# A planned two-layer kernel: own memory for the scans' rows, streamed first-expert weights, and a re-timed plan

## The chip, the cores and the metric

The kernel runs on one core of a Trainium2 chip. The metric is the time of one execution on the device, in microseconds; times of several runs are given by their median. A profile shows one execution in detail.

The engines are named as in the profile: PE (matrix multiply, with PEld for its weight loads), DVE (vector), ACT (activations), POOL (GpSimd), and SP, which here only issues DMA transfers. Each engine runs its own instructions in their order and waits for the others by semaphores.

## The reference, cut to what matters

Sixteen batches of 256 tokens with 128 features go through two layers. Each layer has an attention-like part and experts; norms, shifts, scales and gates stand around them.

```python
# layer 0, attention part: retention with 8 heads, decay g per head
S = g * S + k_t[..., :, None] * v_t[..., None, :]
y_t = einsum('bhde,bhd->bhe', S, q_t)            # then a group norm and Wo
# layer 0, experts: each of 8 experts chooses 64 tokens of each batch
top_p, top_idx = top_k(softmax(x @ gate_w)ᵀ, 64)
y = gelu(xin @ w1) @ w2 * top_p                  # added back to the chosen tokens
# layer 1, attention part: a selective scan, 256 channels x 16 states
dA = exp(dt_t[..., None] * A)
h = dA * h + dt_t[..., None] * b_t[:, None, :] * u_t[..., None]
y = einsum('bdn,bn->bd', h, c_t)                 # + u*D, times silu(z), W_out, layer norm
# layer 1, experts: each token chooses 2 of 8 experts
out = sum_k weight_k * (silu(x @ w1_k) * (x @ w3_k)) @ w2_k
```

All of it is float32.

## The kernel before

**The planner.** The kernel is not written in its final order. Each piece of work is a *chain* of operations with an urgency (`pl.chain(U[...])`, lower numbers first). A chain can `need` results, `take` tokens that stand for buffers, and `give` them back. `Plan.issue` keeps a clock for each engine and repeatedly chooses the next operation: of those that could start within 0.15 us of the earliest one on that engine, the one of the most urgent chain. The order in which it emits them becomes the fixed order of each engine. The durations that it uses come from the formulas of `_us`, or from a `us=` at the call; a DMA's time to land from `_lag`. It plays no part on the chip: at run time only the order and the semaphores remain. Nearly all operations are recorded through one helper, so most have line L119 in the profile and are told apart by tile names.

**Retention** (`retention(g)`, four groups of four batches). `scores` makes the norm, `pqk`, `pv`, and four score tiles `sc` with products `pr`; `outputs0` makes `py` and `yT`; `project` makes `po`; `expert_scores` makes `gs`; `choose` runs eight rounds of `V.max` and `match_replace` on `wk` and ends with `done(("slot", g))`. The scores of the four `j` use four PSUM banks of their own (`ps_d`'s two, `ps_c`, `ps_y`).

**First experts** (`experts_of(q)`, four passes of four batches). `gather` builds one-hot `gg` and `px`; `hidden` multiplies with `fw1` into `ph` and applies gelu to `hg`; `outputs` multiplies with `fw2` into `pye` and copies to `ysb`; `scatter` reads rows `gt` and `pr` from DRAM and adds `pos` to the residual, ending with `done(("x0", b))`. `fw1` and `fw2` are loaded once, 2 MB each, from ACT's queue, and stay in memory.

**Scans.** `front(b)` makes the norm, `bt`, `pxs`, `u`, `pdt` and the softplus, and writes `dx` to DRAM as `dd`. `scans()` holds 256 units, 16 for each batch. Per pair of units SP reads a 512 KB row tile `rep` (three buffers). ACT makes `dA` (exponential, two PSUM tiles), POOL `dB` (twelve buffers), DVE the scan `h` and its product with `ct` (written over `dB`), and PE sums eight products at a time into `ya`. `back(k)` makes `pom`, its layer norm `om`, and the residual (`x1`).

`begin()` opens the memory pool `ml` of the scans' rows after closing the retention's pool, and runs `scans` and `back`; it is hooked on the last group's choice:

```python
pl.after([("slot", 3)], begin)
```

**Second experts.** `prepare(k)` makes `ph`, `hs`, `gbh` and the logits `pl`; `route(g)` ranks tokens (groups of batches (0-3), (4-7), (8-13), (14-15)); `send(g)` scatters rows `disp` by indirect DMA from POOL; `expert(g, j)` works on 128-row tiles, 92 in all: `xt`, `px`, `pa`, `pg`, `sl`, `pm`, `mT`, `py`, `yt`, `ydr`; `combine(k)` gathers `got` and writes `acc`. The weights `w1`, `w3`, `w2` are loaded in `second()`, which is hooked on all `x0`.

Of the kernel before, what the change touches and what calls it, by code (L numbers as in the profile page):

```python
# [31 lines left out]
U = dict(A=-15, AS=0.05, setup=-15.2, E=(-15.5, -12.700000000000001, -13.3, -10.2), Eh=-0.5, Eo=1.5, norm=-16,  # L32
         front=-15, gates=-14, rep=-20, exp=-20, dB=-18.5, ct=-20, sum=-20, scan=5, yg=-16, back=-15, prep=-22,
         route=-22, send=-28.0, tile=-12, comb=-11, wts=-20, depth=2, gap=1.3, wlag=25)
# [58 lines left out]
class Plan:  # L93
# [15 lines left out]
    def _engine(self, key, real):  # L109
        plan = self  # L110

        class Engine:
            def __getattr__(self, name):
                def call(*args, us=None, lag=None, **kw):
                    if us is None:
                        us = plan._us(key, name, args, kw)
                    if lag is None:
                        lag = plan._lag(name, args, kw)
                    return plan.op(key, us, lambda: getattr(real, name)(*args, **kw), lag)  # L119

                return call

        return Engine()
# [139 lines left out]
def adaln_two_layers(ctx: ExitStack, tc: tile.TileContext, a: dict, out: bass.AP):  # L263
# [25 lines left out]
    pe = phase.enter_context(tc.tile_pool(name="pe", bufs=1, side="right"))  # L289

    ma = ctx.enter_context(tc.tile_pool(name="ma", bufs=1))
# [56 lines left out]
    fw1 = fixed(r1, [P, E, HF], "fw1")  # L348
    fw2 = fixed(r1, [P, E, 4, D], "fw2")
    iota0 = fixed(r1, [P, CAP], "iota0")  # L350
    slot_tok = fixed(r1, [P, NCH, B, E], "slot_tok")
    lcol = fixed(r1, [P, 1], "lcol")
# [35 lines left out]
    pl.tokens(hTa=4, an=8, xna=2, q=2, v=2, kd=1, pr0=1, pr1=1, pr2=1, pr3=1, yT=6, tabA=4, yn=2, res=1)  # L388
    pl.tokens(w=2, e=2, va=1, vg=1, vx=1, vy=1, ct=2, ya=1)
    pl.tokens(xin=4, xnq=1, gg=2, gt=2, pr=1, hg=2, ysb=4, fres=1, tab0=1, fn=2)  # L390
    pl.tokens(hT=5, bt=3, th=1, u=3, dx=1, spy=1, spl=1, sz=2, yg=2, om=1)
    pl.tokens(xn2=1, hTf=1, sq=1, hs=4, hs0=2, gbh=1, tab1=1, tab2=1, tab3=1, acc=1, got=3)
# [75 lines left out]
    def retention(g):  # L468
# [17 lines left out]
        own = ((ps_d, "dA0", "va"), (ps_d, "dA1", "vg"), (ps_c, "c", "vx"), (ps_y, "y", "vy"))  # L486
        side = "e"
# [3 lines left out]
        up = U['A'] + U['AS'] * g  # L491
        p_tok = at.tile([P, NCH, 4, E], F32, tag="p_tok", name=f"p_tok{g}")

        def feature_major(b, which, nb, rs, i, name):
# [4 lines left out]
            take("hTa", 2)  # L499
# [21 lines left out]
        def scores(b):  # L521
# [13 lines left out]
            give("hTa")  # L535
# [29 lines left out]
            take(side)  # L565
            T_.matmul(pk[:, 0, :], hT[:, 0:P], wk, start=True, stop=True, us=0.25)
# [33 lines left out]
        def outputs0(b):  # L600
# [17 lines left out]
            yT = yTs[b] = at.tile([P, L], F32, tag="yT", name=f"yT{b}", bufs=6)  # L618
# [38 lines left out]
        def project(b):  # L657
# [4 lines left out]
            yn = at.tile([P, L], F32, tag="yn", name=f"yn{b}")  # L662
# [16 lines left out]
        def expert_scores(g):  # L679
# [5 lines left out]
            for i in range(4):  # L685
# [8 lines left out]
                give("hTa", "hTa")  # L694
# [61 lines left out]
    pl.chain(-20)  # L756
    need(("an", 0))
    S.dma_start(fw1, a["fw1"].rearrange("p (e h) -> p e h", e=E), us=0.35)
    S.dma_start(fw2, a["fw2"].rearrange("p (e h c) -> p e h c", e=E, h=4), us=0.35)
# [129 lines left out]
    def gather(b):  # L889
# [21 lines left out]
        take("w")  # L911
# [10 lines left out]
        give("w")  # L922
        done(("xin", b))

    def hidden(q):
# [8 lines left out]
        for e in range(E):  # L934
            for hp in range(2):
                pool, tag, tok = own[2 * (e % 2) + hp] if q == 0 else (ps_w, "w", "e")
                ph = pool.tile([P, 2, 4 * CAP], F32, tag=tag, name=f"ph{q}_{e}_{hp}")
                banks[e, hp] = ph, tok
            for hp in range(2):
                take(banks[e, hp][1])  # L940
                for hh in range(2):
                    hc = 2 * hp + hh
                    T_.matmul(
                        banks[e, hp][0][:, hh, :], fw1[:, e, hc * P : (hc + 1) * P],
                        xin[:, e].rearrange("p b l -> p (b l)"), start=True, stop=True, us=0.43,
                    )
            done(("ph", q, e))
# [12 lines left out]
    def outputs(q):  # L960

        for ep in range(4):
# [3 lines left out]
            ysb = ysbs[q, ep] = rf.tile([P, 4, D], F32, tag="ysb", name=f"ysb{q}_{ep}", bufs=4)  # L966
            take("ysb")
            take("w")
            for bi in range(4):
                for hc in range(4):  # L970
                    for e2 in range(2):
                        T_.matmul(
                            py[e2 * CAP : (e2 + 1) * CAP, bi, :],
                            hgs[q, 2 * ep + e2][:, hc, bi * CAP : (bi + 1) * CAP], fw2[:, 2 * ep + e2, hc, :],
                            start=(hc == 0), stop=(hc == 3), us=0.127,
                        )
            give("hg", "hg")
# [4 lines left out]
    def scatter(q):  # L982
# [3 lines left out]
        tab = tab0s[q] = rf.tile([P, 4, D], F32, tag="tab0", name=f"tab0_{q}")  # L986
        take("tab0")
        Q.dma_start(tab, rowd0[4 * q : 4 * q + 4, D : 2 * D].unsqueeze(0).to_broadcast([P, 4, D]))
        for bi in range(4):
            b = 4 * q + bi  # L990
            gt = gts[b] = rf.tile([P, 4, L], F32, tag="gt", name=f"gt{b}", bufs=2)
            pr = rf.tile([P, 4, L], F32, tag="pr", name=f"pr{b}", bufs=1)
            if b:
                need(("gt", b - 1))
            take("gt")
            take("pr")
            for i, t in enumerate((gt, pr)):
                for e2 in range(2):
                    rows = spd[b // 4].rearrange("(b e k) (i t) -> i b k e t", e=4, k=2, i=2)[i, b % 4, e2]
                    Q.dma_start(t[e2 * CAP : (e2 + 1) * CAP], rows.unsqueeze(0).to_broadcast([CAP, 4, L]), lag=9.0)  # L1000
            V.scalar_tensor_tensor(gt, gt, lcol, pr, ALU.is_equal, ALU.mult, us=1.3)
            give("pr")
            done(("gt", b))
        pl.chain(U['E'][q] + U['Eo'])
        for bi in range(4):
            b = 4 * q + bi
            need(("gt", b), *(("ysb", q, ep) for ep in range(4)))
            po = mbank([P, NCH, D], f"pos{b}")
            take("w")
            for ch in range(NCH):  # L1010
                for ep in range(4):
                    T_.matmul(
                        po[:, ch, :], gts[b][:, ep, ch * P : (ch + 1) * P], ysbs[q, ep][:, bi, :], start=(ep == 0), stop=(ep == 3),
                        us=0.24,
                    )
            give("gt")
            if bi == 3:
                give("ysb", "ysb", "ysb", "ysb")
            t = rf.tile([P, NCH, D], F32, tag="fres", name=f"fres{b}")
            take("fres")  # L1020
            V.tensor_tensor(t, po, both(tab[:, bi, :]), ALU.mult)
            give("w")
# [8 lines left out]
    def front(b):  # L1031
# [10 lines left out]
        hT = hTs[b] = ma.tile([P, DC - 1 + L], F32, tag="hTm", name=f"hTm{b}", bufs=5)  # L1042
# [10 lines left out]
        bt = bts[b] = ma.tile([P, 2, L], F32, tag="bt", name=f"bt{b}", bufs=3)  # L1053
# [220 lines left out]
    def prepare(k):  # L1274
# [30 lines left out]
        for i in range(2):  # L1305
# [4 lines left out]
            if i == 1:  # L1310
                give("w")
# [367 lines left out]
```

## Time and profile before

| what | value |
|---|---|
| three runs, us | 1384.59, 1396.2, 1391.0 (median 1391.0) |
| the profiled execution | 1367.15 us, span 1365.4 us |
| mean granted TensorE clock | 0.873 |
| PE busy | 1054.5 us, 77% |
| DVE busy | 933.8 us, 68% |
| ACT busy | 772.2 us, 57% |
| POOL busy | 760.0 us, 56% |
| moved by DMA | 143.45 MB, mean 105 GB/s |
| scan steps `h` | first at 330.6 us, last at 1128.9 us |

The span runs from the first to the last instruction; the execution's own time has a little more around it. The median of the three runs is 1.7% above the profiled execution, so differences within the profile are to be read against its own 1367.15 us. Busy shares are averages over stages with different limits; the prediction cuts the span into stages.

### The profile page before, as it was taken

Reading aid. Unit: us, or ns where it says so; the run is one execution under the profiler, and the core shown is the slowest. Engines: PE = TensorE matmul, PEld = TensorE weight load, DVE = VectorE, ACT = ScalarE, POOL = GpSimd, SP = SyncE. Lnnn points to the kernel's source line nnn. Section 1 sums busy time; section 2 is a strip of 40 time slices with the busy share of each in tenths; the row PEclk is TensorE's granted clock in tenths of the full one; section 3 lists DMA queues with packets and bytes.
Section 4 is the critical chain, followed back from the end, with each engine's and each line's share of the span. In section 5 each row is a group of like instructions: output and inputs, shape, how many; then the busy total and the mean of one; then the engine's idle time right before and its main releaser. Section 6 shows DMA issues by size and latency. Waiting matters only on the chain.

```text
span 1365.4 us, 20311 instructions
## 1 busy us (share of the span) xinstructions
PE 1054.5 (77%) x6227; PEld 711.7 (52%) x6227; DVE 933.8 (68%) x1844; ACT 772.2 (57%) x1641; POOL 760.0 (56%) x1241
## 2 busy tenths in 40 slices
PE   5997999988777778577645778777668768889993
PEld 4776678666546545255422444445334445556662
DVE  3576545644888888676995989988899894533341
ACT  2344453256659766668455666667776553444452
POOL 3223112134565776857786877878768876450074
PEclk9898898799879988888875988988798899989997
DMA  8124300323547457333667534535435431221132
GB/s 265 14 68 120 72 11 1 72 70 95 131 117 170 108 128 166 83 84 102 171 173 212 143 102 118 157 87 148 120 106 148 111 104 54 64 80 39 38 94 58
DMA packets 108442, 143.45 MB, mean 105 GB/s; under 512 B 15864, under 2 KB 86592, under 8 KB 107712
## 3 DMA queue, kind: packets, MB, share of 16 engines
q1 hardware_dynamic: 102800, 122.06, 34.7%
q0 software_dynamic: 4256, 9.18, 2.4%
q10 hardware_dynamic: 1280, 10.90, 2.2%
q8 instruction: 53, 0.87, 0.3%
q14 instruction: 53, 0.43, 0.1%
HBM read 115.06 MB, written 27.04 MB: 104 GB/s over the span
## 4 chain that ended last, share of the span: by engine, by line
PE 32%; DVE 25%; POOL 15%; ACT 11%; issue 8%; DMA 7%; DVEq 0%; POOLq 0%; ACTq 0%; SPq 0%
DVE h L119 9%; POOL dB L119 5%; DMA rep<-dd 5%; DVE dB L119 4%; PE py L1494 3%; PE pa L1464 3%; ACT L119 3%; PE sc L119 3%; ACT dA L119 3%; PE pg L1464 3%; PE pxs L119 2%; PE ya L119 2%; PE py L119 2%; DVE sl L119 2%; PE pye L119 2%
## 5 line engine op out<-in xcount | busy, mean ns | idle before, releaser
L119 POOL TENSOR_TENSOR dB<-rep,bt 128x512 f32<-128x512 f32 x256 | 326.7, 1296 | 132.7 <-DMA rep<-dd 74.3
L119 DVE TENSOR_TENSOR_SCAN h<-dA,dB 128x512 f32<-128x512 f32 x256 | 314.7, 1229 | 75.9 <-ACT dA L119 54.5
L119 ACT ACTIVATE dA<-rep,A 128x255 f32<-128x255 f32 x512 | 241.5, 476 | 152.4 <-DVE h L119 138.4
L119 DVE TENSOR_TENSOR dB<-h,ct 128x512 f32<-128x512 f32 x256 | 176.2, 688 | 6.5
L119 PE MATMUL ya<-dB,c 128*32 128x512 f32 x512 | 87.2, 724 | 65.5 <-DVE dB L119 65.3
L1494 PE MATMUL py<-w,mT 112*128 x736 | 106.9, 291 | 31.0 <-ACT mT L119 25.2
L1494 PEld LDWEIGHTS py<-w,mT 112*128 112x128 f32 x736 | 96.3, 199 | 63.8 <-ACT mT L119 37.7
L119 POOL DMA_INDIRECT got<-ydr,pos x64 | 61.5, 961 | 109.7 <-ACT mT L119 78.1
L119 DVE SCALAR_TENSOR_TENSOR sl<-sl,pa 128x448 f32<-128x448 f32 x92 | 56.6, 615 | 90.6 <-ACT sl L119 90.6
L1464 PE MATMUL pa<-w,xT 128*128 x184 | 97.8, 616 | 15.3 <-DVE sl L119 5.9
L119 ACT ACT_TABLE_LOAD x74 | 94.9, 1283 | 1.3
L1464 PE MATMUL pg<-w,xT 128*128 x184 | 92.8, 588 | 0.3 <-DVE sl L119 0.3
L119 PE MATMUL ph<-xin,fw 128*128 128x256 f32 x256 | 70.3, 421 | 21.9 <-ACT hg L119 11.8
L1412 POOL DMA_INDIRECT disp<-hs,pos x64 | 64.1, 1001 | 32.4 <-DVE pos L119 16.6
L119 PE MATMUL pye<-fw,hg 128*64 128x128 f32 x1024 | 73.4, 297 | 6.7 <-ACT dx L119 3.2
L119 PE MATMUL pxs<-hTm,wcv 128*128 128x256 f32 x256 | 77.7, 448 | 0.0
L119 ACT COPY mT<-pm 112x512 f32<-112x512 f32 x92 | 53.5, 583 | 37.0 <-PE pm L119 36.9
L119 PEld LDWEIGHTS pye<-fw,hg 128*64 128x64 f32 x1024 | 64.0, 150 | 18.5 <-issue 6.6
L119 PEld LDWEIGHTS ya<-dB,c 128*32 128x32 f32 x512 | 15.9, 124 | 107.8 <-DVE dB L119 75.1
L119 PE MATMUL pm<-c,sl 128*112 128x128 f32 x368 | 59.5, 283 | 15.0 <-DVE sl L119 9.8
L119 PEld LDWEIGHTS ph<-xin,fw 128*128 128x128 f32 x256 | 51.3, 210 | 36.1 <-ACT hg L119 14.0
L119 POOL TENSOR_TENSOR qd<-q,c 128x128 f32<-128x128 f32 x16 | 7.6, 473 | 107.6 <-ACT q L119 107.6
(293 smaller groups left out, 2213.5 us busy)
## 6 DMA issues: line engine op xcount, KB each, us to landing
rep<-dd SPq DMA_DIRECT2D x128, 512.0 KB, 4.5
gt<-spd SPq DMA_DIRECT2D x32, 256.0 KB, 4.8
pr<-spd SPq DMA_DIRECT2D x32, 256.0 KB, 5.7
dd<-dx SPq DMA_DIRECT2D x16, 512.0 KB, 3.8
xt<-disp SPq DMA_DIRECT2D x92, 64.0 KB, 1.9
ydr<-yt SPq DMA_DIRECT2D x92, 64.0 KB, 1.8
w<-in_w ACTq DMA_DIRECT2D x3, 1792.0 KB, 17.3
fw<-in_fw ACTq DMA_DIRECT2D x2, 2048.0 KB, 8.5
```

The source lines that it names most:

```text
L119: return plan.op(key, us, lambda: getattr(real, name)(*args, **kw), lag)
L1412: i = nc.gpsimd.indirect_dma_start(out=disp[g], out_offset=bass.IndirectOffsetOnAxis(ap=pos[g][:, c, r, :], axis=0), in_=hss[GROUPS[g][c / ...
L1464: nc.tensor.matmul(o, xT, w[:, bass.ds(which[0], 1), :].rearrange("p o i -> p (o i)"), start=True, stop=True)
L1494: nc.tensor.matmul(py, mT[:, ic, :], w2[:, bass.ds(which[0], 1), ic, :].rearrange("p o d -> p (o d)"), start=(ic == 0), stop=(ic == NFC - 1),)
```

## The change

The change touches where buffers lie, which event opens the scans, how the first experts' weights arrive, which tiles are copied out of PSUM, and the planner's numbers.

1. The scans' pool `ml` is opened beside the retention's from the start. `scans` and `back` move from `begin` to a new `recur`, hooked on the scores of retention group 1 (`EARLY = 2`) and all `hg` of pass 0. Retention groups 2 and 3 use the shared PSUM pool `ps_w` with the two tokens `e` for their scores.
2. `fw1` and `fw2` become 32 tiles each per kernel (expert by expert, for each of the four passes), 256 KB apiece, loaded from SP, with 2 and 4 buffers.
3. `ysb`, `tab0`, `gt`, `pr`, `fres` lie in a pool `rw` that the second experts share for `hs`, `acc`, the tables and `got`. `gt` and `pr` are halved. Buffers of `yT` go from 6 to 4, `yn` 2 to 1, `hTm` 5 to 4, `bt` and `u` 3 to 2.
4. `om` and `hs` are copied out of PSUM by ACT first; statistics, `gbh` and `hs` then read the copy.
5. `w1` and `w3` are loaded in `begin`, `w2` in `second`, which is hooked on the last pass's `ysb`.
6. The planner looks up durations in a table `USUAL` by engine, tile and size, and all urgencies `U` are new.

```diff
-U = dict(A=-15, AS=0.05, setup=-15.2, E=(-15.5, -12.700000000000001, -13.3, -10.2), Eh=-0.5, Eo=1.5, norm=-16,
-         front=-15, gates=-14, rep=-20, exp=-20, dB=-18.5, ct=-20, sum=-20, scan=5, yg=-16, back=-15, prep=-22,
-         route=-22, send=-28.0, tile=-12, comb=-11, wts=-20, depth=2, gap=1.3, wlag=25)
+U = dict(A=(-27.35, -16.05, -15.45, 46.6), setup=-34.65, E=(-42.15, 39.3, 75.0, 33.85), Eh=-43.75, Eo=-49.25,
+         norm=34.2, front=-6.85, gates=-73.15, rep=-27.35, exp=-15.05, dB=91.6, ct=32.55, sum=6.05, scan=87.0,
+         yg=38.9, back=-20.75, prep=-42.55, route=12.25, send=-52.55, tile=23.35, comb=38.9, wts=23.25,
+         depth=2, gap=1.3, wlag=25, fw=27.7)
+
+USUAL = {
+    "S": {("A", 32): 0.189, ("xna", 128): 0.411, ("hTa", 256): 0.515, ("q", 256): 0.355, ("ko", 256): 0.444,
...
+                    us = USUAL.get(key, {}).get((short, out.free_size()), us)
                     return plan.op(key, us, lambda: getattr(real, name)(*args, **kw), lag)
...
     ma = ctx.enter_context(tc.tile_pool(name="ma", bufs=1))
+    ml = ctx.enter_context(tc.tile_pool(name="ml", bufs=2))
+
+    rw = ctx.enter_context(tc.tile_pool(name="rw", bufs=1))
...
-    fw1 = fixed(r1, [P, E, HF], "fw1")
-    fw2 = fixed(r1, [P, E, 4, D], "fw2")
+
+    NF1, NF2 = 2, 4
+    fw1s, fw2s = {}, {}
...
+    EARLY = 2
+    TPX, TPO = "w", "w"
+    NYT, NHT, NBT, NU, NGT = 4, 4, 2, 2, 3
...
         own = ((ps_d, "dA0", "va"), (ps_d, "dA1", "vg"), (ps_c, "c", "vx"), (ps_y, "y", "vy"))
+        if g >= EARLY:
+            own = ((ps_w, "w", "e"),) * 4
...
-    pl.chain(-20)
+    pl.chain(U['fw'])
     need(("an", 0))
-    S.dma_start(fw1, a["fw1"].rearrange("p (e h) -> p e h", e=E), us=0.35)
-    S.dma_start(fw2, a["fw2"].rearrange("p (e h c) -> p e h c", e=E, h=4), us=0.35)
+    for q in range(4):
+        for e in range(E):
+            f1 = fw1s[q, e] = r1.tile([P, HF], F32, tag="fw1", name=f"fw1_{q}_{e}", bufs=NF1)
+            f2 = fw2s[q, e] = r1.tile([P, 4, D], F32, tag="fw2", name=f"fw2_{q}_{e}", bufs=NF2)
+            take("f1")
+            Q.dma_start(f1, a["fw1"].rearrange("p (e h) -> p e h", e=E)[:, e])
+            take("f2")
+            Q.dma_start(f2, a["fw2"].rearrange("p (e h c) -> p e h c", e=E, h=4)[:, e])
+            done(("fw", q, e))
...
+            for half in range(2):
+                gt = gts[b, half] = rw.tile([P, 2, L], F32, tag="gt", name=f"gt{b}_{half}", bufs=NGT)
+                pr = rw.tile([P, 2, L], F32, tag="pr", name=f"pr{b}_{half}", bufs=1)
...
-        nb, rs = scales([po[:, i, ch, :] for i in range(2) for ch in range(NCH)], f"o{k}")
         o = ma.tile([P, 2, NCH, D], F32, tag="om", name=f"om{k}")
+        S.copy(o, po)
+        give("w")
+        nb, rs = scales([o[:, i, ch, :] for i in range(2) for ch in range(NCH)], f"o{k}")
...
+        S.copy(hs, ph)
+        give("w")
...
-            V.tensor_tensor(t, ph[:, NCH * i : NCH * (i + 1), :], both(tab[:, i, :]), ALU.mult)
-            if i == 1:
-                give("w")
+            V.tensor_tensor(t, hs[:, NCH * i : NCH * (i + 1), :], both(tab[:, i, :]), ALU.mult)
             G.tensor_tensor(X[b], X[b], t, ALU.add)
             give("gbh")
+        for i in range(4):
+            V.tensor_scalar(hs[:, i, :], hs[:, i, :], rr[:, i : i + 1], None, ALU.mult)
...
-        w1 = fixed(fw, [P, E, FI], "w1")
-        w3 = fixed(fw, [P, E, FI], "w3")
...
     def begin():
-        nonlocal ml, pb
+        nonlocal pb, w1, w3
         before.close()
-        ml = ctx.enter_context(tc.tile_pool(name="ml", bufs=2, reuse_waits="tile"))
-        scans()
-        for k in range(NB):
-            back(k)
 
         pb = ctx.enter_context(tc.tile_pool(name="pb", bufs=1, reuse_waits="tile"))
+        w1 = fixed(pb, [P, E, FI], "w1")
+        w3 = fixed(pb, [P, E, FI], "w3")
...
+    def recur():
+        scans()
+        for k in range(NB):
+            back(k)
+
+
+    pl.after([("pr", 4 * EARLY - 1, j) for j in range(4)] + [("hg", 0, e) for e in range(E)], recur)
     pl.after([("slot", 3)], begin)
...
-    pl.after([("x0", b) for b in range(B)], second)
+    pl.after([("ysb", 3, ep) for ep in range(4)], second)
```

## The prediction

> **What bounds the kernel now.** I read the windows view first, cut where the scan steps begin (first `h` at 330.6 us), at the starts of batches 4, 8 and 12 (529.3, 750.1 and 937.6) and after the last sum (1132.8).
>
> ```profile
> core 0: us, PE busy (x) PEld busy (x) DVE busy (x) ACT busy (x) POOL busy (x), PEclk, DMA share, GB/s
> 0.00:331.00 331.00, 291.19 (x2219) 221.67 (x2219) 172.79 (x568) 132.09 (x273) 80.01 (x269) 0.90 0.29 77
> 331.00:529.00 198.00, 149.59 (x924) 102.08 (x924) 168.50 (x216) 145.74 (x266) 131.49 (x163) 0.87 0.53 132
> 529.00:750.00 221.00, 140.37 (x776) 91.06 (x780) 168.05 (x292) 138.65 (x266) 158.16 (x245) 0.78 0.53 141
> 750.00:938.00 188.00, 144.72 (x666) 83.96 (x658) 164.87 (x275) 129.50 (x292) 144.36 (x207) 0.88 0.46 123
> 938.00:1133.00 195.00, 144.51 (x668) 84.15 (x669) 173.99 (x302) 122.89 (x289) 152.69 (x220) 0.86 0.45 120
> 1133.00:1365.00 232.00, 184.13 (x980) 128.80 (x979) 85.58 (x195) 103.36 (x260) 93.29 (x142) 0.93 0.22 60
> ```
>
> Three stages with three limits. Head (0 to 331): PE 88% busy, DVE half idle. Scan stage (331 to 1133): DVE 85, 76, 88 and 89% busy, PE 64 to 77%. Tail (1133 to 1365): PE 79% busy, DVE half idle again. So a serial DVE stage stands between two PE stages, and what can be laid over it pays. Next, the groups and DVE's waits in the scan stage (total, times, longest):
>
> ```profile
> L119 DVE TENSOR_TENSOR_SCAN h<-dA,dB 128x512 f32<-128x512 f32 x256 | 314.7, 1229 | 75.9 <-ACT dA L119 54.5
> L119 DVE TENSOR_TENSOR dB<-h,ct 128x512 f32<-128x512 f32 x256 | 176.2, 688 | 6.5
> L119 POOL TENSOR_TENSOR dB<-rep,bt 128x512 f32<-128x512 f32 x256 | 326.7, 1296 | 132.7 <-DMA rep<-dd 74.3
> L119 ACT ACT_TABLE_LOAD x74 | 94.9, 1283 | 1.3
> ...
> DVE h L119 <- ACT dA L119: 54.5, 29, 4.7
> DVE hs L119 <- POOL iy_r L119: 11.9, 6, 7.6
> DVE om L119 <- ACT om L119: 9.6, 5, 6.2
> DVE h L119 <- POOL dB L119: 2.0, 1, 2.0
> ...
> rep<-dd SPq DMA_DIRECT2D x128, 512.0 KB, 4.5
> ```
>
> A scan unit costs DVE 1.229 + 0.688 = 1.917 us, 256 units 491 us. DVE's idle time is mostly ACT being late with the exponential, because ACT runs in order and stands at something else. POOL waits for rows, DVE hardly ever for POOL. The chain agrees: DVE 25%, POOL 15%, ACT 11% of the span, PE 32% mostly in head and tail.
>
> **The change part by part.** The arithmetic barely changes; the order does. I took both orders, engine by engine, gave each instruction its group's mean in the profile (PE: its share of the busy time), and added up DVE's work:
>
> before: ahead of the first `h` 170; batches 0-3, 4-7, 8-11, 12-15: 162, 167, 168, 175; after the last 86.
> after: ahead 135; 176, 178, 182, 181; after the last 79.
> PE, to and from the sums `ya`: before 316 ahead, 200 behind; after 252 ahead, 176 behind.
>
> **Earlier start.** The scans no longer wait for the last group's choice (`slot` 3) but for the second group's scores and the first experts' gelu. In the new PE order the fourth first-layer result (`pos` of batch 3) ends at 190 us of PE work; PE had done that much by 218.8 us. Before, the same matmuls ended at 283.4 and the first scan came 47 us later (norm chain, front, `dd` 3.8 us, `rep` 4.5 us). 219 + 47 gives 266; the chain held some waits for the last choice, so I take a first scan at **262**, 68 us earlier. The cross-check: the first sum has 252 us of PE work ahead, which PE had done at 286.7; eight units of about 2.5 us before it put the first scan at 267.
>
> **What this adds to the scan stage.** 716 us of DVE work in place of 672: the last groups' `pr` (12 x 0.684), 20 search steps (`wk`, `m`: 11.5) and their company. What each quarter cost over its DVE work before: 198/162 = 1.22, 221/167 = 1.32, 188/168 = 1.12, 195/175 = 1.12. The first, third and fourth factors I keep: 214 + 203 + 202. In the second all engines were low together (near 717 to 751 us DVE was busy 20 of 34): ACT and POOL stood in an order that didn't fit. The planner now gets measured durations, which should repair part of this; I take half the excess, 1.275: 227. Sum **846** us.
>
> **Tail.** Tiles left after the last sum: 54 before, 47 after. Before, 232 us for 200 us of PE work; 7 tiles at 3.43 us (ten in a 34 us slice) leave 24 less: **208**. The last group's route and send took until 1215, 83 us after the last sum; 118 us of PE work now stand ahead of its first tile, so they stay covered.
>
> Sum: 262 + 846 + 208 = **1316**, against a span of 1365.4: -49 us.
>
> **The small edits**, all inside that sum.
> - ACT: 16 copies (`om`, `hs`) at 0.58 us, as `ct` 0.580: +9.3. Table loads 75 to 83, and 64 to 75 within the scans. Here the Trainium skill speaks against the change (ScalarE: Activation LUTs, "What ACT_TABLE_LOAD costs"): every switch is a load of 1283 ns plus a drain of about 1380. The row has the 1283; the drain I don't find: at 299.06 us the load starts as the work before it ends, and the next activation starts 0.01 us after it. Eight more cost 10.3 us by the row, 21.3 by the rule; I take the row. ACT has 250 us to spare in the scan stage; where a load stands ahead of `dA`, DVE waits.
> - `hs`, `gbh`, `st_o` read SBUF copies in place of PSUM. SBUF - State Buffer, "Who interferes with whom": a DVE instruction with two SBUF inputs, or a tensor_scalar in a two-port mode, locks against GpSimd for whole instructions. Rows: `gg` 0.684 us alone, 1.284 in the scan stage; `spd` 0.427 alone, 0.676 there. By the rule 48 instructions behind a 1.3 us `dB` on an engine 73% busy there: 45 us. By the rows 0.25 each: 12. I take 12, less 5 from the 11.9 us wait of `hs` for `iy_r`, now behind `gbh`; below: -10.
> - First experts' weights: two 2 MB loads become 64 of 256 KB on SP, 12.6 MB more. Queue q1 took 474 us for 122 MB, so +49 us of transfer, spread over some 450: the DMA share goes from 0.53 to about 0.64. No row is the same; 256 KB took 2.4 (`out`) to 4.8 us (`gt`). With two `fw1` buffers, the closest reuse (pass 1, expert 0 to 2) has 2 us of PE work between, the others 4 or more: 3 us exposed once, 0 to 25 over all, on a PE that doesn't bind. I take 3.
> - Half-size `gt`, `pr`: 16 x 1.47 becomes 32 x 0.75 us of DVE. SP gets 64 more issues at 0.6 us: 38 us, on a queue that waited 429 us for ACT.
> - Last two groups' scores on two banks: nothing, to 32 x 0.68 = 22 us of PE, under the scans. Fewer `bt`, `u`, `hT`, `yT`: depth is two batches anyway; 0 to 15. Early `w1`, `w3`: ready long before the first tile; 0.
>
> I leave these out beyond the factors: +13 at my values, inside what the old factors hold, from -15 to +60.
>
> **Rivals.**
> A. The new order fits everywhere: all four quarters at 1.117. 716 x 1.117 = 799; span 1269. For it: half the stage already runs so. Against: retention and experts in the first half have longer chains.
> B. The gain is given back: both first quarters at 1.32, and ACT's 20 us straight on DVE's path: 468 + 203 + 202 + 20 = 893; span 1363. For it: DVE's waits are for ACT, which gets more. Against: `dA`'s own 138 us of waiting for DVE.
> C. **Slower: weight loads block the row loads on SP.** In the new SP order 22 of the 32 weight pairs stand between `rep` loads, each behind PE's release of a buffer. SP runs in order: if PE is late, `rep` waits behind them, then `dB`, then the scan. If each pair holds a `rep` back by one landing (4.5 us): 99 us; span 1415. It decides from 11 of 22 pairs. For it: POOL waits 74 us for rows already. Against: 3 `rep` buffers and 12 `dB` buffers lie between, and DVE waited 2.0 us for `dB`.
>
> **How the numbers follow.** The profiled execution took 1367.15 us for a span of 1365.4; the median of the runs is 1391.0, so I scale spans by 1391.0/1365.4: forecast 1316 to **1341**, A 1293, B 1389, C 1442. Chances: forecast 0.45, A 0.20, B 0.20, C 0.15. About 1% (1377 to 1405) is what a measurement tells from no change. Faster: the first two and some of B, 0.71; same: most of B and C's mild end, 0.14; slower: C, 0.15. The range takes in A and B and leaves most of C: 1285 to 1395.
>
> **What would show it.** Right: first `h` near 262, last near 1108, 47 tiles after it, quarters near 214, 227, 203, 202. Wrong if `h` starts after 300, if DVE waits for `dB` by more than 20 us (C), if DVE's wait for `dA` grows past 90 (B), or if `gbh` and `hs` pass 0.8 us each.

## The result, and the profile after

The changed kernel takes 1375.1 us in the median of 4 runs (1374.09 to 1377.36), the kernel before beside it 1391.5 us: ratio 0.990, 95% interval 0.986 to 0.993. Two later comparisons, on different chips, gave 0.995 (0.990 to 0.999) and 0.986 (0.981 to 0.990). Weighted by the inverse square of their half-widths, the three make **0.990**, some 14 us. By these intervals the mean would be good to 0.0024, but the three lie further apart than the intervals allow; 0.005 is the safer figure. The sign and the range of the prediction held; the size did not: 16 us in place of 50.

The windows view of the kernel after, cut at its own first `h`, at the starts of batches 4, 8 and 12, and after the last sum:

```profile
core 0: us, PE busy (x) PEld busy (x) DVE busy (x) ACT busy (x) POOL busy (x), PEclk, DMA share, GB/s
0.00:276.00 276.00, 245.02 (x1733) 183.35 (x1733) 136.79 (x442) 106.30 (x215) 68.29 (x231) 0.88 0.33 94
276.00:490.00 214.00, 178.30 (x1096) 120.96 (x1094) 177.78 (x284) 154.92 (x281) 128.47 (x165) 0.85 0.51 142
490.00:714.00 224.00, 159.35 (x888) 103.73 (x888) 186.31 (x322) 154.13 (x293) 151.52 (x222) 0.78 0.54 151
714.00:933.00 219.00, 174.81 (x865) 112.52 (x861) 188.89 (x320) 145.93 (x322) 163.72 (x264) 0.87 0.50 131
933.00:1160.00 227.00, 168.59 (x789) 104.00 (x790) 191.24 (x315) 138.90 (x322) 164.03 (x229) 0.86 0.40 109
1160.00:1376.00 216.00, 163.19 (x866) 115.63 (x864) 77.46 (x181) 93.31 (x236) 84.88 (x133) 0.92 0.21 58
```

Head 331 to 276, tail 232 to 216, scan stage 802 to 884. The head's lead of 55 us is more than used up by a scan stage that grew by 82. In the stage every engine has more to do: PE 579 to 681 us, DVE 675 to 744, ACT 537 to 594, POOL 587 to 608.

The groups of the same lines on the page after, and VectorE's waits between 276 and 1160 us (total, times, longest):

```profile
L174 POOL TENSOR_TENSOR dB<-rep,bt 128x512 f32<-128x512 f32 x256 | 326.0, 1295 | 161.3 <-DMA rep<-dd 77.9
L174 DVE TENSOR_TENSOR_SCAN h<-dA,dB 128x512 f32<-128x512 f32 x256 | 314.6, 1229 | 72.0 <-ACT dA L174 37.2
...
L174 DVE TENSOR_TENSOR dB<-h,ct 128x512 f32<-128x512 f32 x256 | 175.9, 687 | 6.1
...
L174 ACT ACT_TABLE_LOAD x82 | 105.2, 1283 | 1.5
```

```profile
DVE h L174 <- ACT dA L174: 37.2, 21, 4.9
DVE h L174 <- POOL dB L174: 13.7, 8, 3.4
DVE sl L174 <- ACT sl L174: 10.0, 5, 5.3
DVE om L174 <- ACT om L174: 9.1, 5, 5.0
```

The scan step itself is as it was, and VectorE waits less for `dA` than before. No single wait of VectorE has grown that would explain 82 us. That is why the experiments ask what a microsecond of work on each engine is worth in this stage.

### The profile page after: what moved, and what is told of

The parts are those of the page before. It is cut to its first block, busy times and chain, and to the rows that moved or that the text cites. A ratio compares the mean times of both kernels' runs of the same rounds, so it can differ in the third digit from the quotient of the medians.

```text
span 1375.6 us, 20606 instructions
## 1 busy us (share of the span) xinstructions
PE 1089.2 (79%) x6227; PEld 740.2 (54%) x6227; DVE 958.5 (70%) x1860; ACT 793.5 (58%) x1665; POOL 760.9 (55%) x1241
## 4 chain that ended last, share of the span: by engine, by line
PE 37%; DVE 26%; POOL 15%; ACT 10%; issue 8%; DMA 3%; DVEq 0%; another core or an unknown queue 0%; POOLq 0%; SPq 0%; ACTq 0%
DVE h L174 10%; PE sc L174 4%; DVE dB L174 4%; PE py L1576 4%; PE pye L174 3%; PE pa L1546 3%; ACT L174 3%; POOL dB L174 2%; PE pg L1546 2%; ACT dA L174 2%; PE ph L174 2%; PE ya L174 2%; PE py L174 2%; POOL got L174 2%; PE px L174 2%
## 5 line engine op out<-in xcount | busy, mean ns | idle before, releaser
L174 POOL TENSOR_TENSOR dB<-rep,bt 128x512 f32<-128x512 f32 x256 | 326.0, 1295 | 161.3 <-DMA rep<-dd 77.9
L174 ACT ACTIVATE dA<-rep,A 128x255 f32<-128x255 f32 x512 | 241.0, 475 | 145.3 <-DVE h L174 133.4
L174 DVE TENSOR_TENSOR dB<-h,ct 128x512 f32<-128x512 f32 x256 | 175.9, 687 | 6.1
L1576 PE MATMUL py<-w,mT 112*128 x736 | 113.1, 302 | 46.9 <-ACT mT L174 39.6
L1576 PEld LDWEIGHTS py<-w,mT 112*128 112x128 f32 x736 | 101.4, 209 | 79.5 <-ACT mT L174 52.8
L174 PE MATMUL ya<-dB,c 128*32 128x512 f32 x512 | 88.9, 687 | 30.4 <-DVE dB L174 30.4
L174 ACT ACT_TABLE_LOAD x82 | 105.2, 1283 | 1.5
L174 PEld LDWEIGHTS pye<-fw,hg 128*64 128x64 f32 x1024 | 67.1, 158 | 16.6 <-ACT hg L174 6.3
L174 PE MATMUL pxs<-hTm,wcv 128*128 128x256 f32 x256 | 70.9, 423 | 0.0
L174 ACT ACTIVATE yt<-py 128x128 f32<-128x128 f32 x92 | 25.1, 273 | 77.2 <-PE py L1576 59.0
L174 DVE TENSOR_TENSOR sl<-sl,pg 128x448 f32<-128x448 f32 x92 | 57.1, 621 | 10.1 <-DVE sl L174 0.9
```

The costliest lines, as they stand in the source:

```text
L1576: nc.tensor.matmul(py, mT[:, ic, :], w2[:, bass.ds(which[0], 1), ic, :].rearrange("p o d -> p (o d)"), start=(ic == 0), stop=(ic == NFC - 1),)
```

## The experiments

All ratios are to the kernel before, run on the same chip in the same comparison.

### How far one profile can be trusted: e1, e5, e17

e1 is the kernel before once more, e5 and e17 the kernel after.

> The kernel before, unchanged, for a second profile: its one profile took 1367 us while its timed runs took 1385 to 1396. If that profile was an unusually quick execution, this one takes about 1391 with the same scan stage start (near 331 us) and 15 to 25 us more spread over the stages; then the change's true gain is the 16 us of the medians. If the profile is typical, it takes 1367 again and the timed runs are slower for a reason outside the program.

> The changed kernel, unchanged, beside the kernel before on one chip and with many runs, as a measure for the other runs. Ratio to before 0.985 to 0.998; scan stage near 884 us with 744 us of DVE work again.

> The changed kernel itself once more, beside the next run, so that the shares of the cuts have a base that is narrower than the two ratios so far (0.990 and 0.995): 0.989 to 0.995 is expected.

Measured: e1 1.001 (0.999 to 1.003), e5 0.995, e17 0.986, which is below the 0.989 expected at the least. The kernel before ran from 1364 to 1385 us in one comparison. Its profile in e1 has a span of 1381.5 us (head 335, stage 813, tail 233), between the two cases that were expected, against 1365.4 in the profile that the prediction was made from: that one shows a quick execution. Whether chance or a quicker chip made it so isn't known. The kernel before had medians of 1378 us on the chips of e1 and e5, and of 1395 to 1398 on the three chips of the later runs; on which chip the first profile was taken isn't recorded. The three profiles of the kernel after have spans of 1375.6, 1365.1 and 1379.5, with first scans at 276, 285 and 280, stages of 884, 873 and 882, and tails of 216, 207 and 218. So a reading of one profile is good to some 10 us in each stage, and what follows rests on ratios to the kernel before on the same chip.

### The parts of the change: e2, e3, e6, e7, e8

e2 is the kernel after with the old urgencies `U` and without the table `USUAL`; e3 is e2 with the scans hooked on the last group's choice again:

```diff
-    pl.after([("pr", 4 * EARLY - 1, j) for j in range(4)] + [("hg", 0, e) for e in range(E)], recur)
+    pl.after([("slot", 3)] + [("hg", 0, e) for e in range(E)], recur)
...
-        if g >= EARLY:
+        if g >= 4:
```

> The changed kernel with the old urgencies and without the table of durations; buffers, gate and streamed weights as changed. Theory P (the new order puts lumps of other work into the second half of the scan stage, which ate the lead of the early start): 1340 to 1360, third and fourth quarter of the scan stage near 203 us each. Rival Q (the second half costs more because more work is there whatever the order, and the new order carries the gain): 1385 or more.

> As e2, and the scans hooked on the last group's choice again, with the last groups' scores on their own four banks: the early start undone under the old order. If the earlier start is worth its lead, 30 to 55 us slower than e2. If a lead in the scans is given back later, within 10 us of e2.

e6 is the kernel before with nothing but the streamed first-expert weights (the `fw1s`, `fw2s` part of the diff), e7 the kernel before with nothing but the measured durations, e8 the kernel after with one number of the planner changed:

```diff
-    SLACK = 0.15
+    SLACK = 0.20
```

> The kernel before with the first experts' weights streamed as in the change (64 transfers of 256 KB on SP, two and four buffers), nothing else changed. Theory S (SP's order makes the small weight loads hold up rows and gates behind PE, which the new urgencies then had to repair): most of the 100 us that the changed kernel lost under the old urgencies appear here, so 1430 to 1480, with SP waiting for PE pye and ph. Rival (streaming is harmless, the loss came from fewer buffers and copies): within 10 us of before.

> The kernel before with the table of measured durations in the planner, old urgencies, old buffers. If measured durations repair the stalls of the second quarter, as the prediction had it: 10 to 20 us faster, the second quarter under 210 us. If the order's fit does not hang on durations this fine: within 10 us either way.

> The changed kernel with the planner's tie width at 0.20 us in place of 0.15: the same work, urgencies and buffers, another order among near-equal choices. It measures how much an order without meaning moves the time. If the tuned order matters in itself: 5 to 30 us slower. If orders of one kind are worth the same: within 5 us.

| run | ratio, 95% | first `h` | scan stage | tiles left in the tail |
|---|---|---|---|---|
| e2 | 1.072 (1.065 to 1.080) | 393.5 | 835 | 46 |
| e3 | 1.079 (1.070 to 1.087) | 384.3 | 866 | 47 |
| e6 | 1.035 (1.030 to 1.040) | 360.1 | 806 | 57 |
| e7 | 1.035 (1.029 to 1.041) | 362.2 | 790 | 65 |
| e8 | 1.013 (1.008 to 1.018) | 286.4 | 908 | 48 |

Three things follow. The new memory, early scans and streaming under the old urgencies cost 7%; the new urgencies and durations together win 8% back. Neither theory of e2 foresaw that: its third and fourth quarters took 216 and 208 us, not the 203 of theory P, and its 1479 us lie far above where rival Q begins. The early hook by itself gives 0.7% there (e3 against e2), which their intervals don't tell from nothing, and e2's first scan comes later than e3's in spite of it. In e2 SP, which issues the row loads as well, stands for PE to release the buffers of second weights, 98 us of it ahead of the first scan. That this makes the first scan late is read from the waits, not tried. From SP's waits in e2 (total, times, longest; in the kernel after this wait is not among the five longest):

```profile
SPq L172 <- PE pye L172: 115.2, 9, 35.1
```

And streaming alone, with the order that the planner then wrote, costs 48 us, not the 3 us of the prediction; that lies between the two cases expected of e6. The windows view of e6 says where, head first:

```profile
0.00:360.00 360.00, 304.98 (x2293) 231.98 (x2293) 174.04 (x570) 143.90 (x285) 81.93 (x271) 0.89 0.32 85
360.00:1166.00 806.00, 555.89 (x2901) 344.75 (x2902) 673.77 (x1074) 524.73 (x1085) 579.61 (x826) 0.83 0.53 137
1166.00:1412.00 246.00, 194.98 (x1036) 136.26 (x1033) 90.22 (x201) 108.78 (x274) 97.72 (x146) 0.94 0.22 60
```

The scan stage is unmoved (806); the head is 29 us longer and the tail 14. e7 and e8 warn against reading this as a price of the transfers alone: durations that the chip never sees cost 3.5%, where a gain or nothing had been expected, and a slack of 0.20 in place of 0.15 costs about 2% against the kernel after (1398.9 against 1368.9 us in the same comparison). Each of these edits makes the planner write another order, and another order by itself cost 48 us in e7 and 30 in e8. The parts can't be priced one by one with the planner between; the runs below therefore keep every engine's order.

### The price of a microsecond on each engine: e9 to e15, e18

In these runs the durations told to the planner are held, so every instruction stands in its old place. One frequent instruction of the scan stage is made shorter, or GpSimd gets one more behind each `dB`. e9 and e11 are the same cut in the kernel after and before: half of the products `dB<-h,ct` are left out of the sums. e10 and e12 are the same addition (shown without the lines that record both instructions as one operation of the plan):

```diff
-V.tensor_tensor(dB, h, cts[b][:, half, :].unsqueeze(1).to_broadcast([P, 2, L]), ALU.mult)
+V.tensor_tensor(dB[:, 0:1], h[:, 0:1], cts[b][:, half, :].unsqueeze(1), ALU.mult, us=0.663)
```

```diff
 nc.gpsimd.tensor_tensor(dB, rep, bt, ALU.mult)
+nc.gpsimd.tensor_scalar(dB[:, 0, 0:64], dB[:, 0, 0:64], 1.0, None, ALU.mult)
```

> The changed kernel with every instruction in its order, but the product dB<-h,ct, 256 times on the vector engine, on the first 256 of its 512 columns (the products of the second half are left out of the sums). By the row res<-po,tabA (128x256, 0.42 us) each should take 0.42 instead of 0.687 us: 68 us less vector work. Theory 1, the scan stage is vector work times a factor of about 1.19 (884 by 744): the stage loses 68 x 1.19 = 81 us, the ratio to before is near 0.935. Theory 2, in the third and fourth quarters another engine (GpSimd with its dB lines and indirect DMAs) paces the stage: only the first half gives its share, 35 to 45 us, ratio near 0.965. Theory 3, order and waits between engines pace it everywhere: under 20 us, ratio above 0.98.

> The changed kernel with every instruction in its order, and behind each of GpSimd's 256 dB<-rep,bt one more GpSimd instruction that multiplies 64 columns of the same tile by 1 (by the row COPY wveo, 128x64, 0.233 us: some 60 us more work on GpSimd, all in the scan stage). Theory 1 (vector work paces the stage): GpSimd's dB lines are done ahead of the scans, cost under 15 us, ratio to before within 0.989 to 1.0. Theory 2 (GpSimd paces the second half): 30 us or more, ratio from 1.01 up, and the wait of h for dB, 13.7 us now, grows by about as much.

> The kernel before with every instruction in its order, but the product dB<-h,ct on 256 of its 512 columns (second half left out of the sums): again 68 us less vector work by the rows. Theory 1: stage 802 x (675 - 68) / 675, 81 us less, ratio near 0.94. If before is paced by other things (waits for dA, 54.5 us of h's idle time), less: 40 us, ratio 0.97. The difference to the changed kernel with the same cut says whether the change made the stage less bound by vector work.

> The kernel before with every instruction in its order, and the same extra 64-column instruction behind each of GpSimd's 256 dB<-rep,bt: some 60 us more GpSimd work. In before h waited 2.0 us for dB in all, so GpSimd runs ahead: theory 1 and 2 both expect under 10 us here, ratio below 1.01; 30 us or more would say that GpSimd was near the bound already in the kernel before.

e13 and e15 leave out half of PE's sums (after and before: 250 and 256 of 512 columns stay), e14 half of the exponentials, e18 makes the cuts of e9, e13 and e14 together:

```diff
-ya[r].rearrange("p g t -> p (g t)"), sels[:, m % 2, :], hC.rearrange("p g t -> p (g t)"),
+ya[r, 0, :250], sels[:, m % 2, :], hC[:, 0, :250],
```

```diff
-V.memset(dA[:, :, 0:1], 0.0, us=0.06)
+V.memset(dA[:, :, :], 0.0, us=0.06)
...
-dAs[half][:, g, 1:], reps[k // 2][:, g, 0, 1:], AF.Exp, scale=A[:, m, half, g : g + 1], us=0.475
+dAs[half][:, g, 1:128], reps[k // 2][:, g, 0, 1:128], AF.Exp, scale=A[:, m, half, g : g + 1], us=0.447
```

> The changed kernel with every instruction in its order, but TensorE's 256 sums ya<-dB on 250 of their 512 columns (the rest is left out): 0.30 us each becomes about 0.15, some 38 us less work on TensorE, all in the scan stage. TensorE's busy time there rose most of all by the change (579 us of 802 to 681 of 884), so theory A, TensorE carries the longer third and fourth quarters, expects half or more of it back: 20 us or more, ratio to before 0.975 or less. Theory B, no engine carries the stage but the order in which five queues wait for one another, expects a share as small as that of GpSimd (3 us of 97): under 8 us, ratio 0.985 or more.

> The changed kernel with every instruction in its order, but the scalar engine's 512 activations dA<-rep,A on 127 of their 255 columns (decays of the other columns are zero): by the slope of the rows (om 128 columns 0.37, dA 255 columns 0.447 us) 0.08 to 0.11 us less each, 40 to 55 us less work on the scalar engine. h waits 37.2 us for dA now and half of the scalar engine's waits are for h, so: theory A (scalar engine carries the stage with VectorE) 20 us or more, ratio 0.975 or less; theory B (loop of waits) 5 to 15 us, ratio 0.98 to 0.987; nothing, ratio 0.99, if the decays are ready ahead of the scans but for the stalls that end with other engines.

> The kernel before with every instruction in its order, but TensorE's 256 sums ya<-dB on half of their columns: again some 38 us less work on TensorE in the scan stage. If TensorE became more of the bound by the change (theory A), the kernel before gives back less than the changed one: under 10 us, ratio above 0.993. If both give back the same, TensorE's share is not what the change altered.

> The changed kernel with every instruction in its order and the three cuts of e9, e13 and e14 at once: half of the products dB<-h,ct on VectorE (69 us), of the sums ya<-dB on TensorE (38 us) and of the decays dA on the scalar engine (54 us) are left out. Alone they gave ratios to before of 0.971, 0.984 and 0.982, against 0.992 for the changed kernel: 29, 11 and 14 us. If the stage is one chain that runs through all engines in turn, so that each engine's work has a share of its own and the shares add, 54 us: ratio 0.953 (0.947 to 0.960). If the cuts remove the same waits (one engine after the other at the bound), less than they add up to: 0.962 or more. If they stand in for one another, so that each was held back by the other two, more: 0.945 or less.

Work is the change of the group's busy time in the profiles. Time is the ratio less that of the uncut kernel (0.990 for the kernel after, 1 for the one before), times 1391 us; the share is time by work. The intervals take the 0.990 as good to 0.0024. But e9, e10, e13 and e14 had no uncut kernel after beside them, and its own three ratios run from 0.986 to 0.995: this base can move all rows of the kernel after together, by 6 us either way.

| run | engine | work, us | ratio, 95% | time, us | share |
|---|---|---|---|---|---|
| e9, after | DVE | 175.9 to 107.4: -68.5 | 0.971 (0.965 to 0.977) | -27 ± 9 | 0.39 |
| e13, after | PE | 88.9 to 50.5: -38.4 | 0.984 (0.980 to 0.988) | -8 ± 7 | 0.21 |
| e14, after | ACT | 241.0 to 186.6: -54.4 | 0.982 (0.978 to 0.986) | -12 ± 7 | 0.22 |
| e10, after | POOL | +100.8 | 0.997 (0.995 to 0.999) | +10 ± 5 | 0.10 |
| e18, after | DVE, PE, ACT | the three | 0.963 (0.958 to 0.968) | -38 ± 8 | |
| e11, before | DVE | 176.2 to 107.6: -68.6 | 0.989 (0.981 to 0.996) | -15 ± 10 | 0.22 |
| e15, before | PE | 87.2 to 49.6: -37.6 | 0.995 (0.994 to 0.997) | -6 ± 3 | 0.17 |
| e12, before | POOL | +100.1 | 1.030 (1.023 to 1.036) | +41 ± 9 | 0.41 |

- e9 and e11 take theory 1 away: the stage is not VectorE's work times a factor. A microsecond off VectorE gives 0.39 in the kernel after (0.30 to 0.48 with the base at 0.986 to 0.995) and 0.22 in the one before, not 1.19. e11 stayed short even of its weaker case of 40 us.
- e10 takes theory 2 away as well. A hundred microseconds more on GpSimd cost 10 (4 to 16 by the base), and the stage itself went from 884 (874 and 882 in the repeats) to 887; `h`'s wait for `dB` grew from 13.7 to 20.8 us only.
- e13 and e14 come out next to and in their weaker case: neither PE nor ACT carries the stage. That each has a share of its own is likely but not shown: with the base at 0.986 their times are 2 and 6 us, inside the intervals of their ratios.
- e15 was compared with its own uncut kernel and shows a share of PE in the kernel before. e13's is about the same, so nothing here says that the change made PE the bound.
- e18 lies on the edge of its second case: the three cuts give 38 us, the sum of the three is 47. But beside e18 ran the uncut kernel after (e17, 0.986), and with that base the three cuts give 31 us and their sum is 28. So the shares roughly add; whether they overlap isn't shown.
- The rows of GpSimd are additions and the others are cuts. What a microsecond more costs need not be what a microsecond less gives.

e12 was a miss for all theories: in the kernel before, a microsecond more on GpSimd cost 0.41, four times what it cost in the kernel after. The row of `h` had waited 2.0 us for `dB`, from which the expectation concluded that GpSimd ran ahead. The chain of waits had GpSimd in it all the same. By engine, the kernel before and then e12:

```profile
PE 32%; DVE 25%; POOL 15%; ACT 11%; issue 8%; DMA 7%; DVEq 0%; POOLq 0%; ACTq 0%; SPq 0%
```

```profile
POOL 31%; PE 29%; DVE 16%; DMA 9%; issue 8%; ACT 6%; another core or an unknown queue 1%; SPq 0%; POOLq 0%; DVEq 0%; ACTq 0%
```

GpSimd's part doubled at VectorE's cost. GpSimd delays VectorE through more doors than `dB`: `hs` waits for its `iy_r`, `om` for an activation that waits for its `nb_o`, the fronts for its `dx`. In e12 the scalar engine's `om` waited 27.8 us for `nb_o`, against 10.7 before. In the kernel after most of the same addition is absorbed: GpSimd's own waits ahead of `dB` for PE's sums fell from 76.8 to 47.3 us and for rows from 77.9 to 38.9. Which part of the change brings this about isn't shown; no run changed the new urgencies alone.

### The copies out of PSUM: e4, e16

Both leave out the 16 copies and let `hs`, `gbh` and `om` read the bank, as in the kernel before. In e4 the planner wrote its order anew; in e16 the copy keeps its place in the plan and issues nothing, so the order stays:

```diff
-        S.copy(hs, ph)
+        pl.op("S", 0.21 + 0.00084 * 512, lambda: None)
...
-            V.tensor_tensor(t, hs[:, NCH * i : NCH * (i + 1), :], both(tab[:, i, :]), ALU.mult)
+            V.tensor_tensor(t, ph[:, NCH * i : NCH * (i + 1), :], both(tab[:, i, :]), ALU.mult)
```

> The changed kernel without the two copies out of PSUM (om, hs): statistics, gbh and hs read PSUM as before; everything else as changed. If the copies cost what the profile shows (gbh and hs 15 us more of DVE, 9 us more of ACT), 10 to 15 us faster than the changed kernel. If freeing the bank early is worth that, the same or up to 10 us slower.

> The changed kernel without its 16 copies of ph and po out of the PSUM banks (hs<-ph, om<-po; hs, gbh, st_o and om read the bank as in the kernel before), with every other instruction in the changed kernel's order, which the earlier try of this edit had not kept. By the groups VectorE loses 15 us (hs 17.4 to 8.9, gbh 12.3 to 5.6) and the scalar engine 10 us. At the share of 0.4 that VectorE's work has shown in the changed kernel: 6 us, and up to 4 more from the scalar engine: ratio to before 0.982 to 0.988 where the changed kernel alone has 0.990 to 0.995. A ratio of 0.99 or more says that the banks held longer cost what the copies did.

The groups by form, before, after, and e16:

```profile
L119 DVE SCALAR_TENSOR_TENSOR gt<-gt,lcol,pr 128x1024 f32<-128x1024 f32 x16 | 23.5, 1467 | 6.6 <-DMA pr<-spd 6.6
...
L119 DVE TENSOR_SCALAR hs<-ph,iy_r 128x128 f32<-128x128 f32 x32 | 9.0, 344 | 17.0 <-POOL iy_r L119 17.0
L119 DVE TENSOR_TENSOR gbh<-ph,tab 128x256 f32<-128x256 f32 x16 | 6.7, 417 | 2.3 <-POOL x L119 2.3
```

```profile
L174 DVE SCALAR_TENSOR_TENSOR gt<-gt,lcol,pr 128x512 f32<-128x512 f32 x32 | 29.3, 915 | 10.4 <-DMA pr<-spd 10.0 <-issue 0.4
...
L174 DVE TENSOR_SCALAR hs<-hs,iy_r 128x128 f32<-128x128 f32 x32 | 18.0, 624 | 0.0
...
L174 DVE TENSOR_TENSOR gbh<-hs,tab 128x256 f32<-128x256 f32 x16 | 13.2, 824 | 10.5 <-POOL x L174 7.9 <-ACT hs L174 2.6
```

```profile
L174 DVE TENSOR_SCALAR hs<-ph,iy_r 128x128 f32<-128x128 f32 x32 | 8.9, 340 | 0.0
...
L174 DVE TENSOR_TENSOR gbh<-ph,tab 128x256 f32<-128x256 f32 x16 | 6.6, 415 | 8.2 <-POOL x L174 5.3 <-ACT sq L174 2.9
```

The durations went back in both. e4 gave 0.996 (0.993 to 0.999), no gain over the kernel after; e16 gave **0.981** (0.978 to 0.984), 12 us better than 0.990; by the shares 16 us of VectorE and 9 of ACT make 8 (6 and 2), within the intervals. The two differ by 1.5%, but they ran on different chips, and the unchanged kernel after has differed by 0.9% from one chip to another: how much of the 1.5% comes of holding the order isn't shown. e16 has the lowest ratio of all versions that compute the whole result. It was not run beside the kernel after.

## Why the prediction was wrong, point by point

**The first scan: 262 forecast, 276 measured (285 and 280 in the other profiles).** PE's part was right: `pos` of batch 3 ended at 209 (218 and 213), where the sum said 219. The step that failed is the chain of 47 us behind it, which took 67. (219 + 47 and the cross-check had given 266 and 267; the 4 us taken off for waits were no help either.) Pieces of the chain of waits of the kernel after, from this `pos` on (start, length, what):

```profile
216.99 1.22 PE pk L174 x4
218.64 1.18 PE sc L174 x4
...
222.32 2.07 PE sc L174 x8
...
226.40 2.00 PE sc L174 x8
...
230.41 2.00 PE sc L174 x8
...
239.61 3.17 PE pxs L174 x12
...
251.56 0.52 ACT spy L174
...
253.39 0.72 ACT spl L174
254.11 0.49 ACT yn L174
...
263.32 1.42 PE sc L174 x14
```

In the kernel before, PE had no scores `sc` left between the first front's links. In the kernel after the fronts run among retention's later groups: their scores `sc` stand between the links on PE, and their `yn` between the softplus steps on ACT. `hTm` came 24 us after `pos` (17 before), the first `spl` 44 (33 before). "47 minus some waits" took a chain's length from a place where this other work was done; the same chain among it is longer. Whether the hook or the new urgencies put it there (`A` of the third group is -15.45, ahead of `front` at -6.85) no run separated: under the old urgencies the chain took 68 us with the early hook (e2) and 81 with the late one (e3).

**The scan stage: 846 forecast, 884 measured.** The first two quarters came out as forecast (214 and 224 for 214 and 227), the last two did not: 219 and 227 for 203 and 202. Two terms of the sum failed.

- *VectorE's work*: 716 forecast, 744 measured. Over the whole kernel it is 958 for 930. The rows above give most of it: `hs` +9.0, `gbh` +6.5, `gt` +5.8 (0.915 us each, where it took 0.75). The prediction named the first two at 12 us by rows and was near (15.5), but left them outside the sum as "inside what the old factors hold". They were not: e16 gets some 12 us back by undoing them (8 by the shares).
- *The factors 1.12*. They were read from quarters in which first-layer work was over. Before, the first layer's last `pos`, of batches 12 to 15, ended between 652 and 702 us, in the second quarter; after, between 732 and 789, in the third. The first pass came 74 us earlier, the second 9, the third was 82 us later and the fourth 87, as read at the end of each pass. The first layer now runs beside later scans, and PE's work in the last two quarters rose from 289 to 343 us. That the early scans push it there is argued, not shown: e3, with the late hook, had its fourth pass end at 950 us and its third and fourth quarters at 216 and 211. Nor is first-layer work the only thing that lengthens a quarter: in e6 it was over at 749, before the third quarter began at 763, and that quarter took 209 all the same.

The common fault is that one engine's work was taken as the stage's price. Stage over VectorE's work is 1.19 before and 1.19 after, so the factor looks confirmed. e9 shows that it describes the stage and prices nothing: with 70 us less work the same stage stands at 858/674 = 1.27. The runs put a share on each engine instead. By the shares, what the stage gained costs 69 × 0.39 on VectorE, 102 × 0.21 on PE, 57 × 0.22 on ACT and 21 × 0.10 on GpSimd: 27 + 21 + 13 + 2 = 63 us, of 82 between the first two profiles and 60 between the repeats e1 and e5. PE and ACT make more than half of it, and the prediction had set them at nothing: "ACT has 250 us to spare", "on a PE that doesn't bind". This sum is an estimate: the shares were measured by cutting other instructions than those that were added, and with the base at 0.986 or 0.995 it is 35 or 90. What is shown is that VectorE's work times a factor doesn't give the stage's time; how the rest divides among PE, ACT and the waits is not.

**The tail: 208 forecast, 216 measured (207 and 218).** The 47 tiles were right. The 8 us are inside what executions differ by.

**The small edits.** Table loads: 74 to 82 at 1283 ns, as the row said; after all but two of them the next activation began 0.01 us later, so no drain stood behind them. The 20 us by which VectorE's waits might have grown did not come. Streaming at 3 us was mis-sized as a step: alone, with its own order, it cost 48, in head and tail, which the prediction had not looked at. The DMA share did not rise to 0.64 either: it was 0.51, 0.54, 0.50 and 0.40 in the four quarters. What streaming costs within the final order was not measured. The repair of the second quarter by measured durations is not shown either: durations alone brought that quarter to 192 us but the third to 210, lost 31 in the head and left 65 tiles for the tail. The "+13 at my values" can't be added up from the terms shown: those given in VectorE's or PE's time make 10 (12 - 5 + 3).

**Rivals.** C did not come: `h` waited 13.7 us for `dB`, under the 20 set for it. B's time (1389) lies nearer to the 1375 than the forecast's, but its mechanism did not come: the lead was given back in the last two quarters instead of the first two, and VectorE's wait for `dA` fell to 37 us instead of passing 90. Of the signs named for "wrong", `gbh` passed 0.8 us, `hs` stayed at 0.62. None of the signs was set on the last quarters, where it went wrong.

**The scaling.** The profile was 1.7% quicker than the median of its runs. Scaling both by one factor kept the difference, but stages read from a quick execution look shorter: head, stage and tail were 335, 813 and 233 in the repeat. That is why the three stages missed by 14 + 38 + 8 = 60 us and the time by only 34 (1375 for 1341): the scaling had added 25, while the profiled execution of the kernel after was no quick one (1377 for a median of 1375).

What stays open: how the 82 us divide, of which a part is the spread of executions; whether early scans with urgencies fitted to them could keep their lead, for no run changed the hook alone under the new urgencies; and why PE is busy 24 us longer in e17 than in e1 (1089.5 and 1065.9 us) with the same 6227 instructions and nearly the same granted clock (0.865 and 0.866).

## What to carry to other kernels

When a stage's engines are all 65 to 85% busy and wait for one another, price a change by all engines' work, not by the busiest one's; a cut of one frequent instruction with the order held measures such a share, if the uncut kernel runs beside it on the same chip. Starting a serial stage earlier over another one did not add the lead to the end here: the displaced work came back inside the stage, and a short dependent chain took 67 us among it in place of 47. With a planner between source and order, compare edits with the order held: one number of the planner moved the time by 2%.

## What the runs showed of the hardware beyond that

- A small GpSimd instruction was dearer in the scan stage than the nearest row. A copy of 64 columns in the head took 0.233 us, the product of 64 columns by 1 here 0.394 in the mean and 0.367 at the least of 256, so waits alone don't make the difference; whether the operation does was not tried:

```profile
L1246 POOL TENSOR_TENSOR dB<-rep,bt 128x512 f32<-128x512 f32 x256 | 327.5, 1279 | 88.5 <-PE ya L174 47.3 <-DMA rep<-dd 38.9 <-DVE u L174 1.2
L1247 POOL TENSOR_SCALAR dB<-dB 128x64 f32<-128x64 f32 x256 | 100.8, 394 | 22.4
```

- Reading the same operand from SBUF instead of PSUM made `hs` 0.28 us and `gbh` 0.41 us longer in the mean, 15.5 us in all. The instructions one by one show why: of the 32 `hs`, 20 took 0.26 to 0.28 us, less than from PSUM (0.34), and 12 took 0.4 to 1.96 us; of the 16 `gbh`, 8 were held up. Each long one ends 0.1 us (`gbh` 0.3) after a large GpSimd instruction with two inputs (`dB`, `dx`, `acc`); beside GpSimd's small ones, of a few columns, none took over 0.48. The views of `hs` in the kernel before and after (shortest/median/longest in ns), then four of them on VectorE and what GpSimd did meanwhile:

```profile
L119 DVE TENSOR_SCALAR hs<-ph,iy_r x32: 327/343/352, 501.4 to 1178.0; 128x128 f32<-128x128 f32 x32
L174 DVE TENSOR_SCALAR hs<-hs,iy_r x32: 261/279/1961, 629.5 to 1208.2; 128x128 f32<-128x128 f32 x32
988.60 4.97 DVE L174 TENSOR_SCALAR hs<-hs,iy_r 128x128 f32<-128x128 f32 x4
988.56 4.93 POOL L174 TENSOR_TENSOR dB<-rep,bt 128x512 f32<-128x512 f32 x4
```

This trace agrees with the rule that the prediction had weighed: the Trainium skill (SBUF — State Buffer, "Who interferes with whom") says that beside GpSimd a `tensor_scalar` in a two-port mode, as `hs` may be, has the ports that both share or waits for them a whole instruction long. The 45 us made of it let 73% of the 48 instructions wait for a whole `dB`; in fact 20 waited, by some 0.9 us each.

- One 128 KB row tile `pr`, at 733.9 us of the kernel after, took 11.0 us to land in the chain of waits, and again 11.1 and 11.7 in e9 and e10, where it started at 725 and 739. In e5, e13, e14, e16 and e17 it took 10.8 to 11.4: it belongs to the order, not to chance.
